# A macaron block on one core: the first expert layer's arrival as a pipeline, three of its batches multiplied beside attention

## The chip, the core and the metric

One core of a Trainium2 chip. The metric is device time of one execution in microseconds (us), the median of several runs. The kernel is written by hand in an explicit order: every engine (TensorE = PE, VectorE = DVE, ScalarE = ACT, GpSimd = POOL, and SyncE = SP, which here only issues transfers) works through its instructions strictly in the order in which the program emits them.

## The reference

x has 8 batches of 512 tokens with 512 channels, float32. Three residual layers follow each other:

```python
x = x + 0.5 * ffn(layernorm(x))
x = x + attn(layernorm(x))
x = x + 0.5 * ffn(layernorm(x))

def ffn(xf):                       # 4096 tokens, 16 experts, one shared weight
    S = softmax(xf @ router_w + router_b)
    G, idx = top_k(S.T, 256)       # each expert takes its 256 best tokens
    out = xf[idx] @ expert_w + expert_b
    return zeros.at[idx].add(G * out)

def attn(x):                       # 16 heads, 4 key/value heads, D = 32, causal
    q, k = rope(x @ Wq), rope(x @ Wk)          # two halves a per head
    s = softmax(mask(q_a . k_a) / sqrt(D))     # a = 0, 1
    diff = softmax(mask(s[0] - lam * s[1]))
    att = rms_norm(diff @ v) * rms_w * 0.2
    return att @ Wo
```

Since all experts share one weight, ffn is one product per token, and a weight per token: the sum of its probabilities over the experts that chose it.

## The kernel before

**Data.** x stays in SBUF as eight tiles `x_sb[b]` of 128 partitions by 4 by 512 (four token tiles i of a batch). `ffn(0)` is the first expert layer, `ffn(1)` the second.

**Arrival (L1019 to L1036).** SP loads x batch by batch, then the choice constants, then attention's weights. For each batch b the loop emits three parts (`arrive`): statistics (`stats`, L236 to L246, DVE and ACT), normalised tiles `xn` (L260, POOL), transposes on PE (L271) that ACT copies to a buffer `y{b}` (L278), router logits (L290), their sums (L303, L310). `expert(count)` puts that many products y x expert weight on PE (L323, four to a token tile), ACT copies the result (L330) and POOL adds the bias row `eb` (L333). Between batches `prepare` lists small work on attention's lambda and output weight (L166 to L188); two of its transfers are asked for in that loop, after all weights.

**Search (`search`, L397 on).** Each expert's threshold is found by 30 bits, one after the other: DVE counts (L420), PE adds the counts over partitions (L424), DVE decides (L427, L428). Beside each bit `expert(per_bit)` keeps PE in work, here 2 or 3 products a bit, and `behind` puts 2 and 4 after the last bit. At the end weights `wt` (L461) say how much of each token's product is added; `update(b, i)` (L464, DVE) does it.

**Preparation (k = -20 to -1).** A table of slots orders this part and attention: `at(o, slot, fn)` places work in block k0 + o, and `fill(k, slot)` emits it. Batch 0 is updated, normalised for attention (`norm_steps`: statistics L488, root L492, shift L496, apply L503, transposes L511) and its first rope products are made (`rope_steps`, PE L563, DVE L572 and L574, a swap of rows by two transfers L580 on SP, POOL L584). The updates of the other seven batches and seven products are spread over its blocks by `PRE_UPDATES` and `PRE_PRODUCTS`.

**Attention (k = 0 on).** 16 phases (batch b, half gp of the heads) of 11 blocks. A block holds 4 x 128 to 4 x 512 scores per partition: `scores` (PE L669, four banks), `energies` (DVE L686: mask added and row minimum), `exps` (ACT L699), in the next block `factors` (L706) and `weigh` (POOL L713 factors, L728 scaling of the odd softmaxes, L735 mask), `difference` (DVE L748), then `exps2` (ACT L762), transposes (`turn_pe` L782, copies L795 on DVE and L797 on ACT), `values` (L810, L825). Rope products and values of the next half, and the output part of the half before (`finish_steps`: squares L599 and L600 on POOL, sums L606, root L617, turned factors `f_f` L625, L633, projection `f_o` L641, residual L647) are placed in slots. The order inside block k:

```python
if u2 is not None: turn_pe(u2)
... values_pe, fill "short", factors, weigh, energies(u)
scores(blocks[k + 1])
... exps2, exps, fill "act mid", fill "mid", turn_copy
fill(k, "long")
... values_out, fill "dve", difference(u1), fill "act", fill "pool"
```

"long" holds the large products on PE (rope, values, projection); what follows them on DVE stands in "mid" of the next block, behind that block's energies. PE has eight PSUM banks: 0 to 3 scores, 4 and 5 transposes, 6 and 7 (`MISC`) in turn for all else.

**Tail.** The second expert layer starts beside the last phase (`EARLY`, `drain`), has its own search with `per_bit` (2,) and `behind` (0, 2), and the outputs leave in 20 transfers.

Of the kernel before, what the change touches and what calls it, by code (L numbers as in the profile page):

```python
# [40 lines left out]
def macaron_kernel(  # L41
# [53 lines left out]


# [14 lines left out]
    def bank(of, name, shape=(P, S)):  # L111
# [6 lines left out]
    PRE_UPDATES = {4: 2, 5: 1, 6: 1, 7: 1, 8: 1, 9: 1, 10: 1, 11: 2, 12: 2, 13: 3, 14: 3, 15: 3, 16: 3, 17: 4}  # L118
    PRE_PRODUCTS = {0: 4, 5: 3}
# [3 lines left out]
        ((0, 0, 1, 1), 1, (2, 2, 3, 3), (3, 3, 4, 4), 5, 6, (5, 6, 7, 8)),  # L123
        ((2, 2, 3, 3), 4, (5, 5, 6, 6), (6, 7, 7, 8), 9, 10, (9, 10, 11, 11)),
# [13 lines left out]
    nlm = keep.tile([P, 2, H], F32, name="nlm")  # L138
    nc.gpsimd.memset(nlm[:, 1, :], -1.0)
    neglam = nlm[:, 0, :]  # L140
# [22 lines left out]
    def lambda_load(n, a, c):  # L163
        def do(pool):
            lqk[n] = [pool.tile([P, H, D], F32, name=f"l{m}t{n}", tag=f"l{m}t") for m in "qk"]
            nc.sync.dma_start(lqk[n][0], a.partition_broadcast(P))  # L166
            nc.sync.dma_start(lqk[n][1], c.partition_broadcast(P))
        return do
# [10 lines left out]
    def lambda_end(wp):  # L179
        nc.gpsimd.tensor_sub(neglam, lsum[1], lsum[0])  # L180
        nc.gpsimd.tensor_scalar(neglam, neglam, -LAM_INIT, None, ALU.add)
# [4 lines left out]
    def scale_wo(q):  # L186
# [8 lines left out]
        0: [lambda_load(0, lq1, lk1)],  # L195
        2: [lambda_products(0)],
        3: [lambda_sums(0), lambda_load(1, lq2, lk2)],
        4: [lambda_exp(0)],
        5: [lambda_products(1), scale_wo_rows],
        6: [lambda_sums(1), scale_wo(0), scale_wo(1)],  # L200
        7: [lambda_exp(1), lambda_end, scale_wo(2), scale_wo(3)],
# [3 lines left out]
    def ffn(f):  # L205
# [3 lines left out]
        buf, mvs, rstds, nmrs, xns, tps, lgps, lgT, lgs, held = ({} for _ in range(10))  # L209
# [4 lines left out]
        def load():  # L214

# [4 lines left out]
            )  # L220
            held["we"] = new("we", "we", [P, EC, E])
# [10 lines left out]
        def stats_tile(b, i):  # L232
            if i == 0:
                mvs[b] = tiny.tile([P, TPB, 2], F32, name=f"mv{f}_{b}", tag="mv")
# [9 lines left out]
        def stats_shift(b):  # L244
            nmrs[b] = tiny.tile([P, TPB], F32, name=f"nmr{f}_{b}", tag="nmr", bufs=3)
            nc.vector.scalar_tensor_tensor(  # L246
                nmrs[b], mvs[b][:, :, 0], -1.0, rstds[b], ALU.mult, ALU.mult
            )

        def stats(b):  # L250
# [3 lines left out]
            stats_shift(b)  # L254

        def normalise(b, tiles=range(TPB), engine=nc.gpsimd):
            first = None
            for i in tiles:
                xns[b, i] = new("xn", f"xn{b}_{i}_", [P, E], bufs=4)
# [919 lines left out]
```

## Time and profile before

| | us |
|---|---|
| median of 7 runs | 1493.42 (1491.14 to 1503.24) |
| profiled execution | 1493.34 |
| its span | 1491.6 |
| arrival, to the last sums | 0 to 80.3 |
| search, to the weights `wt` | 80.3 to 167.3 |
| preparation, to the first energies | 167.3 to 210.9 |
| attention and what lies beside it | 210.9 to about 1303 |
| drain, second search, outputs | 1303 to 1491.6 |

The span runs from the program's first instruction to its last. "Busy" of PE is by records whose ends are modelled; the spacing of their starts tells more. One full product (128x512) is two PE records; a transpose is one. `<-` in a row stands between what is written and what is read, and in brackets stands the idle time of the engine before the row and what ended it. The granted clock is 1.00 or 0.50 at any time; means lie between.

### The profile page before, as it was taken

What the parts mean: (1) busy time and instruction counts of PE and PEld (TensorE: products, weight loads), DVE (VectorE), ACT (ScalarE), POOL (GpSimd) and SP (SyncE); (2) the same over time, 40 slices, a digit from 0 to 9 for tenths busy, and PEclk for the clock granted to TensorE, in tenths of its full rate; (3) what the DMA queues carried; (4) which work ended last, traced back from release to release, by engine and by line L of the source; (5) the groups of instructions that cost most, each with busy time, mean ns of one, the idle gap of its engine ahead of it and who ended that gap; (6) DMA issues with size and microseconds to landing.
All of it is one profiled execution on the core that took longest, in us unless ns stands there. A gap on an engine that the chain in (4) does not pass through costs nothing.

```text
span 1491.6 us, 29871 instructions
## 1 busy us (share of the span) xinstructions
PE 1381.2 (93%) x9496; PEld 780.4 (52%) x9496; DVE 1199.9 (80%) x4440; ACT 1062.5 (71%) x3551; POOL 757.5 (51%) x1241
## 2 busy tenths in 40 slices
PE   6899899999899999999999999999999998999993
PEld 3544444565465555555555555555556555555551
DVE  4345779889989988998899899889988999644467
ACT  3421128988899898889888998988898989733210
POOL 4543435465555655464645555465546455534335
PEclk9999888999999999998999999998999997999996
DMA  9200000000000000000000000000000001000006
GB/s 347 67 0 1 0 36 36 15 23 30 8 30 9 36 2 36 16 22 15 23 19 19 30 8 37 2 36 9 29 16 23 16 23 37 1 5 1 0 1 225
DMA packets 27502, 48.14 MB, mean 32 GB/s; under 512 B 4672, under 2 KB 5968, under 8 KB 27344
## 3 DMA queue, kind: packets, MB, share of 16 engines
q1 hardware_dynamic: 25104, 42.03, 7.8%
q10 hardware_dynamic: 2208, 4.19, 0.8%
q8 instruction: 75, 1.23, 0.3%
q14 instruction: 83, 0.68, 0.1%
q0 software_dynamic: 32, 0.01, 0.0%
HBM read 16.86 MB, written 8.39 MB: 17 GB/s over the span
## 4 chain that ended last, share of the span: by engine, by line
PE 64%; DVE 23%; POOL 3%; ACT 3%; issue 2%; POOLq 1%; DMA 0%; SPq 0%; DVEq 0%; ACTq 0%
PE r_ps L563 13%; PE yps L323 13%; PE sc L669 10%; PE f_o L641 8%; DVE e L686 8%; DVE t L748 6%; PE tp L782 6%; PE av L810 4%; ACT e L699 2%; PE f_ss L606 2%; PE vps L539 2%; DVE eT L795 2%; PE tp L271 2%; PE f_f L625 1%; POOLq L1175 1%
## 5 line engine op out<-in xcount | busy, mean ns | idle before, releaser
L699 ACT ACTIVATE e<-e,nb 128x512 f32<-128x512 f32 (+3 forms) x1024 | 560.4, 551 | 6.9 <-DVE nb L686 2.9
L686 DVE CUSTOM_DVE_ANT_0 e<-sc,mpos 128x512 f32<-128x512 f32 (+3 forms) x1024 | 434.6, 486 | 15.1 <-PE sc L669 7.8
L762 ACT ACTIVATE t<-t,nm 128x512 f32<-128x512 f32 (+3 forms) x512 | 282.2, 554 | 71.8 <-DVE nm L748 71.2
L728 POOL TENSOR_SCALAR e<-e,z,fac 128x512 f32<-128x512 f32 (+3 forms) x512 | 304.7, 607 | 18.3
L669 PE MATMUL sc<-r,r 32*128 32x256 f32 (+3 forms) x2048 | 278.6, 492 | 10.4 <-DVE nb L686 7.2
L748 DVE CUSTOM_DVE_ANT_0 t<-e,fac 128x512 f32<-128x512 f32 (+3 forms) x512 | 254.7, 547 | 13.3 <-POOL e L735 13.2
L323 PE MATMUL yps<-we,y 128*128 128x512 f32 x512 | 248.4, 615 | 0.0
L563 PE MATMUL r_ps<-hT,wq_sb 128*128 128x512 f32 x512 | 236.1, 605 | 0.0
L782 PEld LDWEIGHTS tp<-ident,t 128*128 128x128 f32 x1280 | 154.0, 149 | 112.7 <-issue 36.1
L782 PE MATMUL tp<-ident,t 128*128 128x128 f32 x1280 | 191.5, 291 | 6.4 <-ACT eT L797 5.4
L699 ACT ACTIVATION_READ_ACCUMULATOR e<-e,nb 128x1 f32 x1024 | 194.3, 190 | 0.0
L333 POOL TENSOR_TENSOR y<-y,eb 128x512 f32<-128x512 f32 x64 | 97.8, 1528 | 167.9 <-ACT y L330 146.2
L584 POOL TENSOR_TENSOR r<-r,r_sw 128x512 f32<-128x512 f32 x80 | 101.7, 1279 | 147.0 <-DVE z L706 79.3
L669 PEld LDWEIGHTS sc<-r,r 32*128 32x128 f32 x2048 | 130.2, 195 | 79.5 <-DVE nb L686 55.0
L563 PEld LDWEIGHTS r_ps<-hT,wq_sb 128*128 128x128 f32 x512 | 94.2, 191 | 123.4 <-issue 104.3
L713 POOL TENSOR_TENSOR fac<-z,nlm 128x4 f32<-128x4 f32 (+2 forms) x176 | 36.9, 210 | 232.3 <-DVE z L706 232.3
L330 ACT COPY y<-yps 128x512 f32<-128x512 f32 x64 | 37.4, 585 | 156.7 <-PE yps L323 153.0
L795 DVE COPY eT<-tp 128x512 f32<-128x512 f32 (+1 forms) x176 | 111.8, 635 | 28.1 <-PE tp L782 28.1
L323 PEld LDWEIGHTS yps<-we,y 128*128 128x128 f32 x512 | 90.0, 194 | 84.5 <-issue 81.2
L641 PE MATMUL f_o<-wo_sb,f_an 128*128 128x512 f32 x256 | 126.9, 642 | 0.3
L797 ACT COPY eT<-tp 128x512 f32<-128x512 f32 (+1 forms) x176 | 93.8, 533 | 17.6 <-PE tp L782 17.0
L735 POOL TENSOR_SCALAR_AFFINE_SELECT e<-e 128x256 f32<-128x256 f32 (+1 forms) x224 | 96.0, 439 | 9.4
(110 smaller groups left out, 1630.4 us busy)
## 6 DMA issues: line engine op xcount, KB each, us to landing
r_sw<-r_by SPq DMA_DIRECT2D x160, 128.0 KB, 2.0
x<-in_x_dram SPq DMA_DIRECT2D x7, 1024.0 KB, 14.1
out_dram<-x SPq DMA_DIRECT2D x6, 512.0 KB, 4.0
out_dram<-x ACTq DMA_DIRECT2D x6, 512.0 KB, 4.0
we<-in_expert_w_dram SPq DMA_DIRECT2D x2, 1024.0 KB, 7.2
wq_sb<-in_wq_dram SPq DMA_DIRECT2D x1, 2048.0 KB, 14.2
x<-in_x_dram SPq DMA_DIRECT2D x4, 256.0 KB, 4.6
wo_sb<-in_wo_dram SPq DMA_DIRECT2D x8, 128.0 KB, 2.9
```

What stands on the lines that cost most here:

```text
L323: nc.tensor.matmul(held["yps"], buf[b][:, i, c * P : (c + 1) * P], held["we"][:, c, :], start=(c == 0), stop=(c == EC - 1),)
L563: nc.tensor.matmul(t["ps"], w[:, c, c0 : c0 + P], st["hT"][:, c, :], start=(c == 0), stop=(c == EC - 1),)
L584: return nc.gpsimd.tensor_add(out, out, t["sw"])
L641: nc.tensor.matmul(t["o"], t["an"][:, c, :], wo_sb[:, c // 2, c % 2, :], start=(c == 0), stop=(c == 3),)
L669: nc.tensor.matmul(u["sc"][j][:, r * n : (r + 1) * n], kq[1 + head][j * D : (j + 1) * D, i * P : (i + 1) * P], kq[0][j * D : (j + 1) * D, ...
L686: nc.vector.tensor_tensor_reduce(out=u["e"][:, j, r * n : (r + 1) * n], in0=u["sc"][j][:, r * n : (r + 1) * n], in1=mpos[:, S - n :], scal ...
L699: nc.scalar.activation(e, e, AF.Exp, bias=u["nb"][:, c : c + 1], scale=-1.0, accum_out=u["z"][:, 0, c : c + 1],)
L728: nc.gpsimd.tensor_scalar(e, e, u["z"][:, 1, c : c + 1], u["fac"][:, 0, par, r : r + 1], ALU.mult, ALU.mult,)
L748: u["diff"] = nc.vector.tensor_tensor_reduce(out=u["t"][:, par, s], in0=u["e"][:, 2 * par, s], in1=u["e"][:, 2 * par + 1, s], scale=u["fac ...
L762: nc.scalar.activation(t, t, AF.Exp, bias=u["nm"][:, par, r : r + 1], scale=-1.0, accum_out=z2[:, col : col + 1],)
L782: nc.tensor.transpose(u["tp"][par][:, o : o + P], u["t"][:, par, r * n + c * P : r * n + (c + 1) * P], ident,)
L795: nc.vector.tensor_copy(o, s)
```

## The change

It makes five things different.

1. **Arrival.** The three parts per batch become one pipeline over ten steps: step b emits sums of batch b-2, logits of b-1, apply of b+1, transposes of b, a few products (`BESIDE`: 4 and 2), statistics of b+2. Four banks take the transposes. x1 is loaded before the expert weight, the lambda rows before attention's weights. The shift (L246) goes: the apply subtracts the mean and multiplies.
2. **Search.** `per_bit` (2,) and `behind` (0, 2).
3. **Late batches 4, 5, 6.** Their transposed tiles are kept in `x_sb[b]` itself; their 12 token tiles have no products in arrival and search. A late tile makes four products and one product of a one-row operand that adds the bias, into one bank; SP loads the original x tile again; DVE updates straight from the bank. Five late tiles stand in the preparation, seven in attention, in block 6 of phases 1 to 7. For the latter the expert weight is put in `x_sb[7]`, whose content (already updated) is moved to HBM and comes back in phase 8.
4. **Attention.** `mask` now masks the even softmaxes before `factors`; the factors with lambda are made in place; blocks with four heads use two broadcast multiplies. Squares move from POOL to ACT. "long" is split in two, and scores of the next block stand between or behind the halves in three places (`PLACES`).
5. **Places.** Some positions in `finish_steps`, `EARLY`, `PRE_UPDATES`, `PRE_PRODUCTS` move by a block or so.

```diff
+    LATE = (4, 5, 6)
+    LENT = 7
+    PRE_LATE = (1, 3, 5, 7, 9)
+    LATER = {1: (6,), 2: (6,), 3: (6,), 4: (6,), 5: (6,), 6: (6,), 7: (6,)}
+    BESIDE = {1: 4, 2: 2}
-    PRE_PRODUCTS = {0: 4, 5: 3}
+    PRE_PRODUCTS = {0: 4}
...
-                    xns[b, i], x_sb[b][:, i, :], rstds[b][:, i : i + 1], nmrs[b][:, i : i + 1],
-                    ALU.mult, ALU.add,
+                    xns[b, i], x_sb[b][:, i, :], mvs[b][:, i, 0:1], rstds[b][:, i : i + 1],
+                    ALU.subtract, ALU.mult,
...
+        def late_load(b, i):
+            nc.sync.dma_start(x_sb[b][:, i, :], xt[b][:, i, :])
+
+        def late_pe(b, i):
+            yps = held["late", b, i] = bank(at["y"], f"lps{b}_{i}")
+            for c in range(EC):
+                nc.tensor.matmul(
+                    yps, buf[b][:, i, c * P : (c + 1) * P], held["we"][:, c, :],
+                    start=(c == 0), stop=False,
+                )
+            nc.tensor.matmul(
+                yps, ident[0:1, 0:1].to_broadcast([1, P]), eb_row, start=False, stop=True
+            )
+
+        def late_update(b, i):
+            nc.vector.scalar_tensor_tensor(
+                x_sb[b][:, i, :], held.pop(("late", b, i)), held["wt"][:, i, b : b + 1],
+                x_sb[b][:, i, :], ALU.mult, ALU.add,
+            )
...
+        def late_steps(at, o):
+            b, i = late.pop(0)
+            at(o, "long", lambda: (f0.late_pe(b, i), f0.late_load(b, i)))
+            at(o + 1, "mid", lambda: f0.late_update(b, i))
...
-                first = nc.gpsimd.tensor_mul(t["sq"], st["aT"][i], st["aT"][i])
-                nc.gpsimd.tensor_tensor(t["u"], z2, z2, ALU.mult)
+                nc.scalar.activation(t["sq"], st["aT"][i], AF.Square)
+                nc.scalar.activation(t["u"], z2, AF.Square, scale=RMS_EPS**0.5)
...
-            at(o, "long", lambda: (pe(0), pe(1)))
+            at(o, "long", lambda: pe(0))
+            at(o, "long 2", lambda: pe(1))
...
+        PLACES = (1, 0, 1, 0, 0, 0, 0, 2, 0, 1, 0, 1, 0, 0, 0, 0, 0, 0, 0, 0, 0, 0)
...
             if u1 is not None:
+                mask(u1)
                 factors(u1)
                 weigh(u1)
...
+    for b in range(B + 2):
+        if b > 1:
+            f0.sums_pe(b - 2)
+        if 0 < b <= B:
+            f0.logits_pe(b - 1)
+            f0.logits_put(b - 1)
+        if b + 1 < B:
+            f0.normalise(b + 1, (0, 1), nc.vector if b + 2 == B else nc.gpsimd)
+            f0.normalise(b + 1, (2, 3))
+        if b < B:
+            f0.turn(b, range(TPB))
+        f0.expert(BESIDE.get(b, 0))
+        if b + 2 < B:
+            f0.stats(b + 2)
+        if b > 1:
+            f0.sums_put(b - 2)
+        if b == B:
+            f0.softmax(0)
...
-    f0.search((2, 3), (2, 4))
+    f0.search((2,), (0, 2))
...
+    def lend():
+        if not away:
+            away["x"] = spill.tile([P, TPB, E], F32, name="x_away")
+            nc.sync.dma_start(away["x"], x_sb[LENT])
+            nc.sync.dma_start(x_sb[LENT], expert_w.rearrange("(c p) n -> p c n", p=P))
+
+    def lend_end():
+        nc.sync.dma_start(x_sb[LENT], away["x"])
```

## The prediction

> **What bounds the kernel now.** I read the page first, then busy time by stage, then rows in time order inside each stage.
>
> ```profile
> span 1491.6 us, 29871 instructions
> PE 1381.2 (93%) x9496; PEld 780.4 (52%) x9496; DVE 1199.9 (80%) x4440; ACT 1062.5 (71%) x3551; POOL 757.5 (51%) x1241
> ```
>
> TensorE is 93% busy, but the ends of its records are modelled, so I ask stage by stage. The stages: arrival, search, preparation, attention. Columns: stretch, length, busy time and instructions of PE, PEld, DVE, ACT, POOL, then the granted clock.
>
> ```profile
> 0.00:80.30 80.30, 62.08 (x321) 35.36 (x321) 32.79 (x89) 31.90 (x68) 41.66 (x60) 0.98 0.56 192
> 80.30:167.30 87.00, 86.30 (x257) 42.13 (x257) 50.92 (x169) 13.38 (x24) 32.65 (x27) 1.00 0.00 0
> 167.30:210.90 43.60, 35.20 (x134) 18.40 (x132) 34.70 (x52) 4.49 (x9) 15.78 (x12) 0.84 0.08 31
> 210.90:1303.00 1092.10, 1038.37 (x8052) 600.13 (x8056) 976.71 (x3829) 965.44 (x3350) 589.19 (x1078) 0.94 0.06 21
> ```
>
> The search is PE's own (86.3 of 87.0). In attention PE, DVE (89%) and ACT (88%) run nearly level. Record to record, a full 128x512 product is two records 0.43 us apart, 0.86 us. Summing PE by such spacings gives about 51 of the 67.1 us of the phase 412.6 to 479.7: rope blocks are PE's, but in blocks 4 to 8 of a phase DVE has hardly a gap. There PE has room and DVE has none.
>
> The same line of products, in the bits of the first and of the second search, where the second has 2 products a bit and the first 2 or 3:
>
> ```profile
> 87.90:158.60 70.70, 69.10 (x146) 25.53 (x146) 1.00 0.00 0
> 1399.70:1456.10 56.40, 56.15 (x116) 19.84 (x116) 1.00 0.00 1
> ```
>
> And four rows in time order: a tile load and who waits for it, a POOL wait in the arrival, and DVE held at an output projection:
>
> ```profile
> 0.80 1.80 SPq L1019 DMA_DIRECT2D x<-in_x_dram  x4
> 3.30 0.69 DVE L236 BATCH_NORM_STATS2 s<-x 128x6 f32<-128x512 f32 x1 [2.23 <-DMA x<-in_x_dram]
> 47.58 1.26 POOL L171 TENSOR_TENSOR lqt<-lqt,lkt 128x512 f32<-128x512 f32 x1 [8.18 <-DMA lkt<-in_lk_dram]
> 389.22 0.69 DVE L647 TENSOR_TENSOR x<-x,f_o 128x512 f32<-128x512 f32 x1 [1.83 <-PE f_o L641]
> ```
>
> A 256 KB tile takes 2.5 us from issue to use. DVE, in order, stood 1.83 us because a residual follows a PE projection by one block: late updates will stand in just such a place.
>
> **Arrival: 24.7 us saved.** Products in it fall from 32 to 6: 26 x 0.86 = 22.4 us of PE. What stays is, per batch, transposes 2.1, logits 1.07, sums 0.96: 4.1 us, 4.2 with the evacuations. I place it in order. The first transpose stays at 11.5. The root for batch 1 is now ahead of ACT's copies of batch 0; x1 lands near 12.0 (14.7 less the 2.7 of the megabyte of weights put behind it), four statistics take 3.2, copies end at 18.1, logits at 19.2. Transposes of batch 1 and four products: 24.8. Batch 2 with two products: 30.6. Five batches at 4.2: 51.6. Sums, logits, evacuation, sums of the end: 55.4. Six products 60.6, then 2.6 to the first count: 63.2, where it was 87.9. DVE (3.5 a batch), ACT (3.3) and POOL (3.0) stay under 4.2. POOL's 8.18 us wait goes: the lambda rows are asked for before the weights and used at batch 6; next late is PE itself.
>
> The clock is one uncertainty. It was 0.5 from 49.5 to 52.9, after that wait. But look at 384:
>
> ```profile
> 380.60:384.00 3.40, 3.35 (x34) 2.33 (x34) 3.15 (x15) 3.40 (x13) 3.11 (x5) 1.00 0.03 7
> 384.00:387.40 3.40, 3.40 (x5) 1.32 (x5) 3.26 (x13) 3.36 (x12) 2.01 (x4) 0.50 0.00 0
> ```
>
> Here it halved although PE was 3.35 of 3.40 us busy before, with small transposes and tiled products, which is just what an arrival without products consists of. So I allow four halved stretches of 3.4 us, 1.7 us each: gain 17 to 27. *The Trainium skill ("TensorE: Matmul & The Clock Gate", Part 1) says that the clock halves only after an idle window of about 3.4 us; by that rule the arrival would lose nothing and gain the full 24.7. The row differs, and I follow the row.*
>
> **Search: 14.3 us saved.** 70.7 less 56.4 for the same 29 intervals, DVE's chain being the limit at 2 a bit. Behind the last bit nothing is gained: 8.7 us to the weights in the first search, 8.7 in the second with the new counts.
>
> **Preparation: 16 us lost.** Before, weights at 167.3, ropes from 184.4, attention at 210.9. DVE loses twelve updates of 0.69, but five late tiles come in: each four products and a bias product over one row and 512 columns. No one-row product is in the trace; by the columns it is 0.86, as a full one, so a tile is 4.3 us, five 21.5. PE was idle or waiting for some 10 us here. The chain is DVE's: the second late update stands before the shift (L496) that the normalisation needs. Its reload is behind the lend on SP's queue: x7 away (1 MB, issued near +8.5 us after the weights, 5 us), then the expert weights into its place (5.6 us to landing in the second layer's load), then the reload, landing near +19 to +22 where the shift was done at +8.4. h tiles, two late tiles between the four transposes: ropes start near +35 instead of +17; they then run at full clock, not half, 2.6 us back. Sum +16. If the lend is quicker or hidden, +8; if PE also waits at half clock, +20.
>
> **Attention, seven late tiles: 24 us lost.** One tile at block 6 of phases 1 to 7. In PE's room 4.3 us of products cost little. But DVE's update waits for PE's end, then for SP to reload the tile (2.5): 4.3 + 2.7 = 7.0 us after the scores, and DVE has only about 3.7 us before it (reciprocal, four energies of 0.62, the rest of the block): it stands 3.3. With its own 0.7 that is 4.0, less 0.6 regained where DVE waited anyway: 3.4 a tile, 24 for seven. Behind the standing update are the copy of the transposes, the difference and the next energies, and for them ACT and PE. Ends: 0.7 a tile (5 us) if the wait falls into slack, 7.5 (52) if nothing covers it.
>
> **Attention, the rest: 13 us saved.** The mask now goes before the factors, while POOL waits for the reciprocal (L706). DVE's difference waited for POOL 13.2 us in 25 places (L748 behind L735): I take half, 7. Scores between the halves of the rope products: at 414.5 to 417.2 PE waited for score banks before two ropes; filling that saves about 1.5 in one phase of two, at most 12; I take 10. The squares go from POOL (1.04 each) to ACT: no ACT square is in the trace; its copies of this size take 0.59, exponentials 0.71, with the small one 0.2. 32 x 0.8 = 26 us on an ACT with 12% room; I charge 4, ends 0 and 13. Two broadcast multiplies for eight in 16 blocks are POOL's, off the path. Range of this part: 1 to 21 saved.
>
> **The rest** (the tail's shift, the router load, one reload of x7 in the eighth phase, needed four phases later) I cost at nothing: SP is free there, and the seven reloads come one block after the last rope swaps of a phase (blocks 1 to 5). If any met swaps, 2 to 3 us each.
>
> Sum: -24.7 - 14.3 + 16 + 24 - 13 = -12.0. The profiled execution took 1493.34 (span 1491.6 and 1.7 around it), the median 1493.42: 1481.3 either way. About 0.5% (7.5 us) is what a measurement here can tell from no change: faster is below 1486, slower above 1501.
>
> **Rivals.** *The late updates stall DVE in full (slower).* The place is block 7 of phases 1 to 7, the price per tile. The other terms save 36.0 us, so 5.1 us a tile eats them all, and above 6.2 the kernel is slower by over 0.5%. At 7.5 a tile: +16.5, 1510. For it: in even phases the bank of the late tile is also that of the next turned factors (f_f), so PE waits with DVE; DVE is full there. Against: ACT and PE can run ahead by a block. Chance 0.21.
>
> *The late tiles vanish in the slack.* PE's sum was 51 of 67, and the POOL waits removed lie in those very blocks. At 0.7 a tile, 5 us: 1493.3 - 31 = 1462. Against: DVE has no gap there. Chance 0.22.
>
> *The arrival does not do what it says.* PE at half clock for much of it, or waiting for copies on ACT, 5.6 us a batch instead of 4.2: gain 13, total near 1493, no change. For it: the row at 384. Against: before, with the same small work, only one stretch was halved. Chance 0.17.
>
> My forecast, all terms about as above: 0.40. Faster is this and the second rival, less a little at the edge: 0.60. Same: 0.18. Slower: 0.22. The range goes from just under the second rival, 1460, to 1503, which leaves out the worse half of the first rival and the lower edge of the second.
>
> **What would show it.** The first count at 63 us; its bits 1.94 apart; first energies of attention near 188, with the shift waiting behind a late update; in block 7 of phases 1 to 7 a late update with 2 to 4 us of idle DVE before it, ended by the reload, and phases there 2 to 4 us longer than phases 8 to 14; no L735-like waits before the differences. Wrong if the first count comes after 70, if late updates wait over 5 us, or if attention as a whole is shorter than before.

## The result, and the profile after

The changed kernel takes 1503.08 us (median of 20 runs, 1497.93 to 1509.69) where the kernel before takes 1494.74 (47 runs). The ratio is 1.0054 (1.0043 to 1.0065): 8 us slower, where 12 us faster was forecast. The profiled execution took 1501.66, its span is 8.4 us longer than before:

```profile
span 1500.0 us, 30000 instructions
PE 1388.3 (93%) x9520; PEld 778.7 (52%) x9520; DVE 1194.7 (80%) x4426; ACT 1077.3 (72%) x3603; POOL 746.3 (50%) x1083
```

The shares alone do not tell which engine sets the time. By stage (stretch, length, busy time and instructions of PE, PEld, DVE, ACT, POOL, granted clock), for arrival to the first count, the 29 bit intervals, first update to first energies, and attention to its last energies:

```profile
0.00:84.34 84.34, 59.50 (x288) 36.44 (x289) 36.75 (x94) 29.69 (x64) 75.14 (x58) 0.86 0.55 183
84.34:140.73 56.39, 56.39 (x175) 28.54 (x176) 35.51 (x145) 8.20 (x14) 17.78 (x14) 1.00 0.00 1
147.79:208.25 60.46, 54.63 (x179) 25.55 (x177) 28.95 (x44) 3.92 (x8) 12.35 (x10) 0.92 0.22 78
208.25:1318.50 1110.25, 1059.84 (x8133) 603.83 (x8134) 986.63 (x3845) 989.07 (x3420) 549.47 (x942) 0.96 0.06 23
```

The same stages of the kernel before are 87.9, 70.7, 43.6 and 1095.7 us long. Against before, by the places of the same instructions:

| stage | forecast, us | measured, us |
|---|---|---|
| arrival, to the first count | -24.7 | -3.5 |
| search, 29 bit intervals | -14.3 | -14.3 |
| from the last bit to the first update | 0 | -1.7 |
| preparation | +16 | +16.9 |
| attention | +11 | +14.6 |
| second layer up to its first count | 0 | -2.9 |
| tail | 0 | -0.7 |
| sum | -12.0 | +8.4 |

Of the miss of 20.4 us, 21.2 stand in the first row; the other rows cancel. The first of the prediction's signs of being wrong, a first count after 70 us, came. In the arrival POOL is busy for 75.14 of 84.34 us. POOL in time order, in the middle of the arrival, shows why:

```profile
27.31 4.13 POOL L268 TENSOR_SCALAR xn<-x,mv,rstd 128x512 f32<-128x512 f32 x2
31.41 1.29 POOL L345 TENSOR_TENSOR y<-y,eb 128x512 f32<-128x512 f32 x1
32.67 18.52 POOL L268 TENSOR_SCALAR xn<-x,mv,rstd 128x512 f32<-128x512 f32 x9
```

Nine applies stand back to back, 2.06 us each. The group of this line (ns: least, median, most), the group of the apply in the kernel before, and two rows of the waits of the first 84 us (total, times, longest):

```profile
L268 POOL TENSOR_SCALAR xn<-x,mv,rstd x60: 2062/2075/2347, 9.7 to 1394.8; 128x512 f32<-128x512 f32 x60
```

```profile
L260 POOL TENSOR_SCALAR xn<-x,rstd,nmr x62: 761/769/1029, 10.9 to 1381.8; 128x512 f32<-128x512 f32 x62
```

```profile
PEld tp L279 <- POOL xn L268: 17.7, 15, 1.7
PE tp L279 <- POOL xn L268: 11.1, 9, 1.4
```

With (mult, add) the apply took 0.77 us before. With (subtract, mult) a batch costs POOL 8.3 us, and PE, whose transposes need the tiles, follows at that pace.

In the preparation, SP's queue in time order, and the shift on DVE:

```profile
154.57 0.35 SPq L356 DMA_DIRECT2D x<-in_x_dram  x1
155.64 0.35 SPq L1152 DMA_DIRECT2D x_away<-x  x1
159.91 0.38 SPq L1153 DMA_DIRECT2D x<-in_expert_w_dram  x1
160.39 3.86 SPq L356 DMA_DIRECT2D x<-in_x_dram  x2
```

```profile
166.18 0.75 DVE L371 SCALAR_TENSOR_TENSOR x<-lps,wt,x 128x512 f32<-128x512 f32 x1 [5.86 <-DMA x<-in_x_dram]
167.50 0.16 DVE L527 SCALAR_TENSOR_TENSOR nmr<-mv,rstd 128x4 f32<-128x4 f32 x1
```

The second reload is issued only behind the loan (L1152, L1153), the late update stands 5.86 us for it, and the shift comes 19.7 us after the first update (147.79). A late tile in attention, block 7 of phase 3, some rows of three engines:

```profile
459.91 1.12 PE L366 MATMUL lps<-eb_row,ident 1*128 1x512 f32 x2
460.06 0.33 SPq L356 DMA_DIRECT2D x<-in_x_dram  x1
462.65 0.75 DVE L371 SCALAR_TENSOR_TENSOR x<-lps,wt,x 128x512 f32<-128x512 f32 x1 [3.06 <-PE f_ss L638]
```

PE's four products before these rows (L362) read the place that the reload overwrites; they end at 459.98, and the reload goes out at 460.06. By 462.65, 2.6 us later, it has landed (the twelve reloads take 2.4 to 2.8). The trace names f_ss as the releaser, a product that has nothing to do with this tile. DVE stands 3.06 us (forecast 3.3).

### The profile page after: what moved, and what is told of

Same layout as the page of the kernel before. It is cut to its first block, busy times and chain, and to the rows that moved or that the text cites. A ratio compares the mean times of both kernels' runs of the same rounds, so it can differ in the third digit from the quotient of the medians.

```text
span 1500.0 us, 30000 instructions
## 1 busy us (share of the span) xinstructions
PE 1388.3 (93%) x9520; PEld 778.7 (52%) x9520; DVE 1194.7 (80%) x4426; ACT 1077.3 (72%) x3603; POOL 746.3 (50%) x1083
## 4 chain that ended last, share of the span: by engine, by line
PE 57%; DVE 24%; ACT 8%; issue 3%; POOL 2%; DMA 1%; DVEq 0%; SPq 0%; POOLq 0%; ACTq 0%
PE yps L335 11%; PE r_ps L595 10%; PE sc L700 9%; PE f_o L671 8%; DVE e L717 7%; DVE t L787 7%; ACT e L730 6%; PE tp L821 4%; PE av L849 4%; PE lps L362 3%; PE f_ss L638 2%; PE vps L570 2%; DVE eT L834 2%; POOL xn L268 2%; DVE x L495 1%
## 5 line engine op out<-in xcount | busy, mean ns | idle before, releaser
L787 DVE CUSTOM_DVE_ANT_0 t<-e,z 128x512 f32<-128x512 f32 (+3 forms) x512 | 259.9, 556 | 4.3 <-POOL e L774 3.7
L774 POOL TENSOR_SCALAR e<-e,z 128x256 f32<-128x256 f32 (+2 forms) x384 | 251.2, 665 | 16.7
L821 PEld LDWEIGHTS tp<-ident,t 128*128 128x128 f32 x1280 | 148.8, 145 | 115.0 <-issue 41.0
L335 PE MATMUL yps<-we,y 128*128 128x512 f32 x416 | 201.8, 614 | 0.7 <-ACT y L342 0.7
L821 PE MATMUL tp<-ident,t 128*128 128x128 f32 x1280 | 184.4, 284 | 9.1 <-ACT eT L836 6.7
L751 POOL TENSOR_SCALAR_AFFINE_SELECT e<-e 128x256 f32<-128x256 f32 (+1 forms) x224 | 99.8, 449 | 120.0 <-ACT e L730 119.1
L268 POOL TENSOR_SCALAR xn<-x,mv,rstd 128x512 f32<-128x512 f32 x60 | 124.3, 2087 | 16.6 <-ACT rstd L257 7.9
L342 ACT COPY y<-yps 128x512 f32<-128x512 f32 x52 | 30.4, 585 | 138.8 <-PE yps L335 138.8
L345 POOL TENSOR_TENSOR y<-y,eb 128x512 f32<-128x512 f32 x52 | 67.1, 1290 | 126.4 <-ACT y L342 103.7
L741 POOL TENSOR_TENSOR z<-z,over 128x4 f32<-128x4 f32 (+2 forms) x176 | 36.1, 205 | 188.0 <-DVE z L739 188.0
L335 PEld LDWEIGHTS yps<-we,y 128*128 128x128 f32 x416 | 72.2, 192 | 64.4 <-issue 60.2
```

Of the source, the lines that this page charges most:

```text
L268: ins = engine.tensor_scalar(xns[b, i], x_sb[b][:, i, :], mvs[b][:, i, 0:1], rstds[b][:, i : i + 1], ALU.subtract, ALU.mult,)
L335: nc.tensor.matmul(held["yps"], buf[b][:, i, c * P : (c + 1) * P], held["we"][:, c, :], start=(c == 0), stop=(c == EC - 1),)
L774: nc.gpsimd.tensor_scalar(e, e, u["z"][:, 1, c : c + 1], u["z"][:, 0, c - nr : c - nr + 1], ALU.mult, ALU.mult,)
L787: u["diff"] = nc.vector.tensor_tensor_reduce(out=u["t"][:, par, s], in0=u["e"][:, 2 * par, s], in1=u["e"][:, 2 * par + 1, s], scale=u["z"] ...
L821: nc.tensor.transpose(u["tp"][par][:, o : o + P], u["t"][:, par, r * n + c * P : r * n + (c + 1) * P], ident,)
```

## Experiments

Sixteen kernels ran. Times are medians; a ratio is against runs of the kernel before on the same chip, with its 95% interval. "First count" is the start of the first count's product. The kernel before, run beside each group of them, had medians of 1493.3 to 1495.7, so medians of different experiments compare to about 2 us.

How far one profile can be trusted: e1, e5 and e6 have the same instructions in attention, and it took 1102.5, 1107.1 and 1106.9 us. By block (from one reciprocal of attention to the next; there is one in each block) the view is sharper. Of 154 blocks, 140 agree between e1 and e5 within 0.06 us; of the rest four differ by 1.6 to 1.75. The traces grant the clock in stretches of 3.41 us, full or half, and 1.7 us is half of such a stretch: what work that PE paces loses when the clock is at half for one. So a total that differs by five us shows little, and the same difference in the same block of every phase shows much.

**e1: the old apply in the changed kernel.**

```diff
+            stats_shift(b)
...
-                    xns[b, i], x_sb[b][:, i, :], mvs[b][:, i, 0:1], rstds[b][:, i : i + 1],
-                    ALU.subtract, ALU.mult,
+                    xns[b, i], x_sb[b][:, i, :], rstds[b][:, i : i + 1], nmrs[b][:, i : i + 1],
+                    ALU.mult, ALU.add,
```

> The changed kernel with one thing undone: the apply multiplies by the root and adds the shift again (the shift is back on DVE), as in the kernel before; pipeline, late tiles and attention stay. Theory A (POOL's subtract-multiply takes 2.08 us a tile instead of 0.77, so that a batch costs POOL 8.3 us and the arrival goes at POOL's pace): POOL falls to 3.1 us a batch, PE is next at 4.2, first count at 63 to 67 instead of 84.3, total 1481 to 1486, faster than before. Rival B (PE at half clock, or waiting for ACT's copies, sets the arrival and POOL only trails it): first count stays at 78 to 84, total 1497 to 1503.

1486.28 us, ratio 0.9939 (0.9917 to 0.9961): faster than before, as theory A had it. But the first count is at 75.1, between the two theories: the apply was the first limit, not the only one. Rows of one batch, in time order (others between them are left out):

```profile
45.48 0.16 DVE L261 SCALAR_TENSOR_TENSOR nmr<-mv,rstd 128x4 f32<-128x4 f32 x1 [3.69 <-ACT rstd L257]
45.56 0.22 DVE L326 TENSOR_TENSOR l<-lg,rb_sb 128x64 f32<-128x64 f32 x1
45.93 1.04 PE L319 MATMUL lg<-sum,lgT 128*128 128x16 f32 x8 [1.64 <-DVE l L326]
48.39 3.08 PE L286 MATMUL tp<-ident,xn 128*128 128x128 f32 x16
50.45 1.75 ACT L294 COPY x<-tp 128x512 f32<-128x512 f32 x3 [0.28 <-PE tp L286]
52.09 0.31 ACT L256 ACTIVATE rstd<-mv,ln_eps 128x4 f32<-128x4 f32 x1
52.73 0.16 DVE L261 SCALAR_TENSOR_TENSOR nmr<-mv,rstd 128x4 f32<-128x4 f32 x1 [3.75 <-ACT rstd L257]
```

Read them as a ring: the shift waits for ACT's root; the evacuation of the sums (L326) stands behind the shift on DVE; PE's next sums wait for that one bank; PE's transposes, ACT's copies of them and ACT's next root follow. One round is 7.25 us here, part of it at half clock (47.3 to 50.7). The shift that the change took out closes this ring. With the same instructions in the arrival, e7 and e8 below have their first counts at 71.5 and 71.7, so the 75.1 is good to some 3 us only.

**e2: the new apply alone in the kernel before.**

```diff
-            stats_shift(b)
...
-                    xns[b, i], x_sb[b][:, i, :], rstds[b][:, i : i + 1], nmrs[b][:, i : i + 1],
-                    ALU.mult, ALU.add,
+                    xns[b, i], x_sb[b][:, i, :], mvs[b][:, i, 0:1], rstds[b][:, i : i + 1],
+                    ALU.subtract, ALU.mult,
```

> The kernel before with the new apply form alone (subtract the mean, multiply by the root; no shift); nothing else of the change. Theory A: POOL's row of the apply goes from 0.77 to about 2.08 us a tile; 30 tiles add 39 us to a POOL that was busy for 41.7 of the first 80.3 us, so the arrival becomes POOL's and the first count moves from 87.9 to 95 to 112; total 1500 to 1518. Rival (the form is slow only beside the busier DVE of the pipeline): the row stays under 1 us and the total within 5 us of before.

1515.88 us, ratio 1.0134 (1.0097 to 1.0171). The row is 2.07 us, the first count at 99.8 instead of 87.9, and attention 10.7 longer. Of that, 5.1 are in the last phase, beside which the second layer's first batches are applied; the rest is mostly in block 1 of odd phases, which depends on the clock (see e10) and not on the form. The slow form needs nothing else of the change.

**e3: six pairs of operations on POOL.**

```diff
+                ops = {1: (ALU.mult, ALU.add), 2: (ALU.subtract, ALU.mult), 3: (ALU.add, ALU.mult),
+                       4: (ALU.mult, ALU.mult), 5: (ALU.mult, ALU.subtract), 6: (ALU.add, ALU.add)}
```

> The kernel before, with another pair of operations in the first layer's apply for batches 1 to 6 (its values are therefore not the reference's; only the rows of the apply are read): 1 (mult, add), 2 (subtract, mult), 3 (add, mult), 4 (mult, mult), 5 (mult, subtract), 6 (add, add). Four POOL tiles each. If the subtraction makes the form slow, batches 2 and 5 take 2.08 us and the others 0.77. If it is the order (a product after a sum), 2 and 3 take 2.08 and the rest 0.77. If only (mult, add) and (mult, mult) have a quick way, 2, 3, 5 and 6 are slow.

POOL's rows in time order, batches 1 to 6, four tiles each, and behind them a single multiplication of the same shape, which is a row of the kernel before too (L188):

```profile
18.23 3.03 POOL L263 TENSOR_SCALAR xn<-x,rstd,nmr 128x512 f32<-128x512 f32 x4 [6.02 <-DVE nmr L246]
...
27.94 8.26 POOL L263 TENSOR_SCALAR xn<-x,rstd,nmr 128x512 f32<-128x512 f32 x4 [3.89 <-DVE nmr L246]
...
37.43 3.02 POOL L263 TENSOR_SCALAR xn<-x,rstd,nmr 128x512 f32<-128x512 f32 x4
...
49.23 3.03 POOL L263 TENSOR_SCALAR xn<-x,rstd,nmr 128x512 f32<-128x512 f32 x4
...
53.45 8.27 POOL L263 TENSOR_SCALAR xn<-x,rstd,nmr 128x512 f32<-128x512 f32 x4
...
62.93 8.29 POOL L263 TENSOR_SCALAR xn<-x,rstd,nmr 128x512 f32<-128x512 f32 x4
...
78.09 3.15 POOL L188 TENSOR_SCALAR wo_sb<-wo_sb,rms_sb 128x512 f32<-128x512 f32 x2
```

None of the three rules that I had written down fits. (mult, add), (add, mult) and (mult, mult) take 0.76 us a tile; (subtract, mult), (mult, subtract) and (add, add) take 2.07; a product alone 1.57. All six have the same operands and the same shape, so the pair itself decides, and (add, mult), which serves a mean whose sign is turned, is a quick one.

**e4: no late tiles in attention.**

```diff
-            for o in LATER.get(ph, ()):
-                late_steps(at, o)
-            if ph == max(LATER) + 1:
-                lend_end()
...
-            if len(updates) == TPB * (LENT - 1 - len(LATE)):
-                lend()
```

> The changed kernel without the seven late tiles in attention (their products, reloads and updates are left out, and with them the loan of the x7 tile; the values of those seven tiles are not the reference's). The prediction's term (3.4 us a tile): 24 us shorter, 1479. Stretches of the two traces by phase (3.7 to 4.4 a tile): 1472 to 1477, phases 1 to 7 down to those of before. Rival (they lie in slack, 0.7 a tile): 1498. In the preparation the reload no longer stands behind the loan on SP's queue: a few us shorter there if the loan held it up, 0 if the late updates themselves did.

1477.34 us, ratio 0.9881 (0.9856 to 0.9905). The total fits the phases' reading only because two parts add: attention is 18.2 us shorter than in the changed kernel, 2.6 a tile, and the preparation 8.1 (52.4 instead of 60.5), the price of the loan on SP's queue. Without late tiles attention is still only 3.6 us shorter than before. By block the price of a tile is higher: block 7 of phases 1 to 7 is 3.5 to 5.4 us shorter than in the changed kernel, and in the odd ones block 8 gives 1.1 to 1.4 back, 24.8 in all or 3.5 a tile (against e1, which has half clock in fewer of these blocks, 22.3 or 3.2). The other 6.6 us are lost elsewhere, much of them in steps of 1.7: e4's attention has 133 us at half clock, the changed kernel's 82.

**e5: e1 with the ring cut.**

```diff
-        if b + 2 < B:
-            f0.stats(b + 2)
         if b > 1:
             f0.sums_put(b - 2)
+        if b + 2 < B:
+            f0.stats(b + 2)
```

> The kernel of e1 with one line moved in the arrival: DVE evacuates the sums of batch b-2 before the statistics and the shift of b+2, not after. Reading of e1's trace: there PE's sums wait for their one bank, which DVE frees only behind the shift, which waits for ACT's root, which stands behind ACT's copies of the transposes that PE has just made: a ring of four engines, 5.8 to 7.6 us a batch. Theory A: with the ring cut PE sets the pace again, 4.2 to 5 us a batch; first count at 64 to 69 (e1: 75.1), total 1476 to 1480. Rival B (PE's halved clock or x's arrival set e1's pace): first count stays within 2 us of 75, total 1485 to 1488.

1476.59 us, ratio 0.9869 (0.9850 to 0.9888); first count at 63.7. PE in time order:

```profile
33.14 1.97 PE L286 MATMUL tp<-ident,xn 128*128 128x128 f32 x16
...
36.94 1.97 PE L286 MATMUL tp<-ident,xn 128*128 128x128 f32 x16
...
40.78 1.97 PE L286 MATMUL tp<-ident,xn 128*128 128x128 f32 x16
```

A batch is 3.8 us, PE's own, and the mean clock over the arrival is 1.00 (e1 0.93, the changed kernel 0.86). Theory A holds. Rival B falls: e5 has the same transfers, and the half clock goes with the waits.

**e6: e5 with the loan behind the last reload of the preparation.**

```diff
-            if len(updates) == TPB * (LENT - 1 - len(LATE)):
+            if k == -20 + max(PRE_LATE) + 1:
                 lend()
```

> The kernel of e5 with the loan of x7 (its way out and the expert weights' way in) issued on SP behind the last reload of the preparation instead of ahead of the second. Theory A (the second late update, and the shift behind it, wait for a reload that stands behind the loan on SP's queue): the stretch from the first update to the first energies falls from 61 to 52 to 54 us, where PE's own work is next; total 7 to 9 below e5. Rival (late tiles' products on PE set that stretch, the loan is hidden): within 2 us of e5.

1469.57 us, ratio 0.9820 (0.9801 to 0.9839), 7.0 below e5. The preparation, first update to first energies:

```profile
126.80:180.90 54.10, 52.36 (x179) 24.54 (x177) 29.08 (x45) 3.92 (x8) 11.10 (x10) 0.97 0.26 88
```

PE is busy for 52.36 of 54.10: the loan was what kept it waiting, and next is its own work, the late products among it.

**e7: e1 without the reloads in attention.**

```diff
-            at(o, "long", lambda: (f0.late_pe(b, i), f0.late_load(b, i)))
+            back = len(late) >= len(LATE) * TPB - len(PRE_LATE)
+            at(o, "long", lambda: (f0.late_pe(b, i), back and f0.late_load(b, i)))
```

> The kernel of e1 without the reload of the seven late tiles in attention (their updates read what lies there, so the values of those tiles are not the reference's); products and updates stay. By the prediction's account (DVE stands because the reload's 2.5 us follow PE's end: 3.3 us of 3.4 a tile) the stand falls to 0.8 and a tile costs 0.7 to 1.5: attention 10 to 15 us shorter, total 1471 to 1476. Rival (the 4.8 us of products on PE, or the bank that they hold, are what a tile costs, and the reload's wait is covered): attention within 4 us, total 1482 to 1487.

1477.24 us, ratio 0.9888 (0.9860 to 0.9916), 9 below e1. In the profile attention is 6.8 us shorter, 1.0 a tile, and DVE's idle time before the late updates of attention is PE's alone:

```profile
its engine sat idle before it (us, times) until:
  DMA x<-in_x_dram: 20.6, 4
  PE lps L373: 8.9, 7
```

(The four are the preparation's.) The stand fell from 3.0 to 1.3 us (means of seven). By block, block 7 of the seven phases got 1.0 to 1.35 shorter, 8.2 us together; the rest are steps of the clock. So a tile got only 1.0 to 1.2 cheaper, and neither account holds as written: this much of a tile is the reload, the rest PE's products (4.7 us of PE in every one) and the update itself.

**e8: the squares back on POOL.**

```diff
-                nc.scalar.activation(t["sq"], st["aT"][i], AF.Square)
+                first = nc.gpsimd.tensor_mul(t["sq"], st["aT"][i], st["aT"][i])
...
-            at(o0, "act", square)
+            at(o0, "pool", square)
```

> The kernel of e1 with the squares of the output part back on POOL (as in the kernel before). The prediction charged 4 us for having them on ACT (ends 0 and 13): by that the total falls to 1482 (1473 to 1486). Rival (ACT has room there and POOL had not): 1487 to 1492.

1488.52 us, ratio 0.9956 (0.9936 to 0.9976), which can't be told from e1. On ACT a square takes 0.63 us, and these 32 cost nothing that shows; the 4 us charged for them did not appear, within the 2 us or so that medians tell.

**e9: the mask late again, in e6.**

```diff
-                mask(u1)
                 factors(u1)
                 weigh(u1)
+                mask(u1)
```

> The kernel of e6 with the mask back behind the scaling of the odd softmaxes on POOL (the order of the kernel before, but still on the even ones). The prediction's term (mask early saves 7 us, half of the 13.2 us that differences waited for POOL): 1476 to 1477. Rival (those waits were covered by others): within 3 us of 1469.6.

1473.05 us, ratio 0.9856 (0.9838 to 0.9874). The differences wait for POOL again, 6.3 us in 17 places (e6: none), but attention is only 0.6 us longer. The medians say 3.5 us, with intervals that just touch. In any case less than the 7 of the prediction: most of what DVE waits there does not lengthen attention.

**e10: the scores' places undone, in e6.**

```diff
-        PLACES = (1, 0, 1, 0, 0, 0, 0, 2, 0, 1, 0, 1, 0, 0, 0, 0, 0, 0, 0, 0, 0, 0)
+        PLACES = (0, 0, 0, 0, 0, 0, 0, 0, 0, 0, 0, 0, 0, 0, 0, 0, 0, 0, 0, 0, 0, 0)
```

> The kernel of e6 with the scores of the next block always ahead of the large products (all PLACES 0), as in the kernel before. The prediction's term (scores between the halves save 10 us, at most 12): 1479 to 1481. Rival (PE's order moves DVE's wait from one place to another): within 3 us of 1469.6. With e9: what the prediction called the rest of attention (13 saved) came out at about 6, so one of the two must fall short.

1486.76 us, ratio 0.9935 (0.9911 to 0.9960): 17 us. Its twelve runs spread from 1479.9 to 1496.5 where e6's four lie between 1467.6 and 1470.0. In the profile attention is 18.5 longer, 16.7 of it in phases 0, 3 and 7. The start of phase 3 in e10, in stretches of 3.4 us, and a like stretch of e6:

```profile
390.60:394.00 3.40, 3.38 (x12) 2.02 (x13) 2.12 (x7) 3.40 (x18) 0.71 (x1) 0.50 0.00 0
394.00:397.40 3.40, 3.40 (x5) 1.35 (x4) 2.76 (x17) 3.40 (x12) 2.83 (x5) 0.51 0.03 7
```

```profile
391.20:394.60 3.40, 3.38 (x14) 1.70 (x12) 3.40 (x18) 3.40 (x12) 2.82 (x5) 1.00 0.01 2
```

With the scores put ahead of all rope products the clock is at half for two stretches in which the big rope products run; with the places it stays full. Block 1, where these products stand, is 4.3 to 4.5 us longer in phases 0, 3 and 7; in phases 1, 9, 11 and 13, with the same order but full clock there, only 0.4 to 0.6 (1.9 in phase 5, where the half clock reaches in for 0.6 us). The three phases have 17.9 us more at half clock than in e6, which can account for 9 of the 16.7 at most. So neither order nor clock alone makes the loss: the old order is expensive where the clock is at half. The kernel before, e2 and e3, whose attention has the old order too, agree: block 1 of an odd phase takes 8.7 to 9.1 us at full clock and 11.6 to 12.7 with 2.4 to 3.9 at half, in phases 7 and 13 of one trace, 3, 7 and 11 of the next, 1 and 11 of the third. With the places it takes 8.25 in every trace but for phase 1 of e4 and e15 (8.61, 8.54); in phase 1 of e13 it takes 8.26 although 3.4 us of it are at half clock.

**e11: late updates in attention in slot dve, in e6.**

```diff
-            at(o + 1, "mid", lambda: f0.late_update(b, i))
+            at(o + 1, "mid" if f0.held["we"] is not x_sb[LENT] else "dve", lambda: f0.late_update(b, i))
```

> The kernel of e6 with the seven late updates in attention a few instructions later on DVE: in slot dve of the same block (behind the two copies of the transposes, ahead of the difference) instead of mid. Reading of e6's block 7: DVE stands for 3.2 us, about 1.5 of it for PE's products and 1.7 for the reload; behind the copies the reload has landed, and the stand shrinks to what PE needs, about 2.2. Theory A (the reload is worth about 1 us a tile, as e7 measured): 5 to 8 us less, 1462 to 1465. Rival (the copy that goes first waits for transposes that PE makes only behind the late products, so that the stand only changes its name): within 3 us of 1469.6.

1467.22 us, ratio 0.9809 (0.9791 to 0.9828); attention as long as in e6. The rows of phase 3:

```profile
431.95 0.56 DVE L841 COPY eT<-tp 128x384 f32<-128x384 f32 x1 [1.95 <-PE tp L828]
433.09 0.75 DVE L378 SCALAR_TENSOR_TENSOR x<-lps,wt,x 128x512 f32<-128x512 f32 x1 [0.59 <-DMA x<-in_x_dram]
```

The update now waits 0.59 us (3.16 in e6), but the copy ahead of it 1.95 for PE's transposes. The stand changed its place: the rival.

**e12: late products split over blocks 5 and 6, in e6.**

```diff
+            at(o - 1, "long", lambda: f0.late_pe(b, i, (0, 1)))
+            at(o, "long", lambda: (f0.late_pe(b, i, (2, 3)), f0.late_load(b, i)))
```

> The kernel of e6 with the late products of attention split: two products in block 5, two and the bias product in block 6; reload and update where they were. PE ends 1.8 us earlier in block 6 and the reload starts earlier. Theory A (what a late tile costs, 2.6 us, is DVE's stand behind PE's end and the reload): the stand falls from 3.2 to 1.4 a tile, 8 to 12 us less, 1458 to 1462. Rival (what a tile costs is PE's own 4.8 us in blocks where PE has little room, so block 5 pays what block 7 saves): within 3 us of 1469.6.

1471.59 us, ratio 0.9835 (0.9815 to 0.9856), attention 0.4 us shorter: the rival again. The stand did fall, from 3.0 to 1.6 us a tile, but block 7 got only 0.3 us shorter a tile. DVE's stand is not what a tile costs.

**e13: the kernel before with the places of the scores and the halves alone.**

```diff
+        PLACES = (1, 0, 1, 0, 0, 0, 0, 2, 0, 1, 0, 1, 0, 0, 0, 0, 0, 0, 0, 0, 0, 0)
...
-            at(o, "long", lambda: (pe(0), pe(1)))
+            at(o, "long", lambda: pe(0))
+            at(o, "long 2", lambda: pe(1))
...
             fill(k, "long")
+            if place == 1:
+                scores_next(k)
+            fill(k, "long 2")
```

> The kernel before with one part of the change: the large products in two halves, and the scores of the next block between or behind them in the places of PLACES. The prediction's term: 10 us saved, at most 12: 1484 to 1487, with the blocks 1 of phases 0, 1, 7, 13, 14 (10.3 to 11.9 us there against 9.0 in like phases) back at 9. If the 17 us that e10 lost by the same places hold here too: 1477 to 1480. Rival (the places only mend what the late tiles and the moved output parts bring about): within 3 us of before.

1479.89 us, ratio 0.9923 (0.9903 to 0.9943): 11 to 13 us. Attention is 14.1 shorter; block 1 of phases 0, 7 and 13, which the expectation named, loses 3.4 to 3.8 each, and these are the blocks that are at half clock in the trace of before. So the places gain without the late tiles too, and a little more than the 10 of the term. But they do not gain as the term was added up, 1.5 us in one phase of two: in phase 3, where the prediction saw PE wait, block 1 loses 0.74.

**e14: the output parts at their old block numbers, in e6.**

```diff
-                    finish_steps(at, (0, 1, 1, 3, 4), b - 1, 2, sts[b - 1])
+                    finish_steps(at, (0, 1, 1, 4, 5), b - 1, 2, sts[b - 1])
...
-                finish_steps(at, (4, 5, 5, 8, 9), b, 0, sts[b])
-                finish_steps(at, (6, 7, 7, 9, 10), b, 1, sts[b])
+                finish_steps(at, (4, 5, 5, 7, 9), b, 0, sts[b])
+                finish_steps(at, (6, 7, 8, 9, 10), b, 1, sts[b])
```

> The kernel of e6 with the output parts back at the block numbers of the kernel before: (0, 1, 1, 4, 5), (4, 5, 5, 7, 9) and (6, 7, 8, 9, 10). Theory (these moves, which the prediction costed at nothing, are what ate the rest of attention's gain: block 8 of odd phases is 2.0 us longer than before without any late tile, block 7 only 1.35 shorter, and the end of block 10 up to 1.7 longer): 4 to 10 us less, 1460 to 1466. Rival (they make way for the late tile's bank, so that without them PE waits for that bank in block 7 and 8): 3 to 15 us more, 1473 to 1485.

1467.48 us, ratio 0.9833 (0.9807 to 0.9860). The profiled execution, the fastest of four, has attention 5.9 us shorter; the medians show no difference. By block the theory has half of it right. Block 8 of phases 9, 11 and 13 falls from 6.4 to 6.7 us, 3.7 to 4.3 of them at half clock, to 4.8 at full clock; block 10 falls by 1.4 to 1.7 in six odd phases, again with the half clock gone. Block 7 grows by 9.6 us over all phases, which speaks for the rival. What the moves are worth in all is not settled.

**e15: the changed kernel with the quick pair.**

```diff
+            if done[b] == TPB:
...
+                nc.vector.tensor_scalar(negs[b], mvs[b][:, :, 0], -1.0, None, ALU.mult)
...
-                    xns[b, i], x_sb[b][:, i, :], mvs[b][:, i, 0:1], rstds[b][:, i : i + 1],
-                    ALU.subtract, ALU.mult,
+                    xns[b, i], x_sb[b][:, i, :], negs[b][:, i : i + 1], rstds[b][:, i : i + 1],
+                    ALU.add, ALU.mult,
```

> The changed kernel with one thing different: DVE writes the mean with its sign turned (128x4 elements, straight behind the statistics, no wait for ACT), and the apply adds it and multiplies by the root. e3 showed (add, mult) at 0.76 us a tile on POOL, so the shift need not come back. Theory (two causes, POOL's form, and in e1 the ring through the shift; this removes both without touching the order): POOL 3.0 us a batch, first count at 62 to 66, total 1474 to 1480, about e5. Rival (the order of the sums' evacuation matters also without the shift, since it stands behind four statistics): first count at 70 to 76, total 1483 to 1488, about e1.

1480.49 us, ratio 0.9910 (0.9876 to 0.9944); first count at 62.7. The group of the apply:

```profile
L272 POOL TENSOR_SCALAR xn<-x,neg,rstd x60: 762/768/1037, 9.9 to 1366.1; 128x512 f32<-128x512 f32 x60
```

Only this is different from the changed kernel, and it is worth some 22 us. Neither the shift nor another order is needed. This is the change as the prediction had priced it: forecast 1481.3 and a first count at 63.

**e16: e15 with the loan of e6 and the slot of e11.**

```diff
+            if k == -20 + max(PRE_LATE) + 1:
                 lend()
...
+            at(o + 1, "mid" if f0.held["we"] is not x_sb[LENT] else "dve", lambda: f0.late_update(b, i))
```

> The kernel of e15 with the loan of x7 behind the last reload of the preparation (as in e6) and the seven late updates in slot dve (as in e11). If these add: 8 us less than e15 by the loan, 0 to 3 by the slot: 1464 to 1471.

1468.89 us, ratio 0.9831 (0.9797 to 0.9865). The loan's gain adds to it. e6, e11, e14 and e16 lie between 1467 and 1470 and can't be told apart; all beat both kernels by 25 us and more.

## Why the prediction was wrong, and where it was right

**The step that failed** is in the arrival: "DVE (3.5 a batch), ACT (3.3) and POOL (3.0) stay under 4.2." The 3.0 was four tiles at 0.77, the row of the old pair, given to a new pair with no bound on either side. It measures 8.3, so the arrival is POOL's: -3.5 instead of -24.7. The trace of before held a warning: a single multiplication of the same shape took 1.57 us, twice the pair with one operation more, so POOL's time did not follow the shape alone:

```profile
L188 POOL TENSOR_SCALAR wo_sb<-wo_sb,rms_sb x4: 1557/1566/1583, 74.4 to 83.8; 128x512 f32<-128x512 f32 x4
```

The slow pair also costs about 2.4 us in the last phase and 1.8 in the second layer up to its first count (changed kernel against e1). The third rival came nearest to this stage (13 gained there instead of 24.7), but by other engines. The half clock that it named was there, 24 us of the changed kernel's arrival; with the quick pair it is gone but for 3.4 us at most (e5, e15), so it followed from the waits for POOL and was not the cause.

**Right:** nearly all else of the arrival. With the quick pair it ends 25.2 us earlier than before (87.9 to 62.7, e15), against 24.7 forecast, and from batch 1 on PE sets the pace. The products of batch 2 end at 30.8 us (forecast 30.6). That it agrees to 0.5 us is partly luck: five batches take 3.9 each and not 4.2, and the end, from the last transposes to the first count, takes a us more than forecast. That removing the shift mattered I had not seen: with it, but in the new order, the engines form a ring (first count 71.5 to 75.1 in e1, e7 and e8, 63.7 in e5).

**The clock in the arrival.** I had allowed four halved stretches, for the row at 380.6. e5 shows none, e15 one (17.4 to 20.8, behind a wait of PE of 3.34 us): small transposes without waits kept full clock. The Trainium skill ("TensorE: Matmul & The Clock Gate", Part 1) would have it so, and for these two its outcome was the better one. The changed kernel does not fit its idle window of about 3.4 us. Two stretches of its arrival, one behind the other:

```profile
64.23:67.64 3.41, 2.22 (x20) 1.67 (x22) 0.00 (x0) 1.43 (x3) 3.41 (x2) 1.00 0.02 5
67.64:71.06 3.42, 3.42 (x20) 2.41 (x13) 0.00 (x0) 1.58 (x3) 3.42 (x4) 0.50 0.00 0
```

The clock halves though PE was busy for 2.22 of the 3.41 us before. At all eight places where it halves in the arrivals of the changed kernel and e1, PE was busy for 0.9 to 2.2 us of the stretch before, and no single wait there was over 1.8 us. So short waits were enough, without a stretch that was idle. In attention the halved stretches stay (e10), some behind stretches in which the records show PE busy for 2.97 (e10) or 3.35 (the row at 380.6) of 3.40 us; no run here shows what sets those off.

**POOL by the page.** In e15's row a quick pair takes 0.768 us for 512 elements in each partition. The Trainium skill ("GPSIMD Engine Reference", section 3.1) gives 769 ns measured for 512 elements in the best case, which agrees; for the 2.07 of the other pairs it has no figure.

**Search and preparation:** -14.3 and +16.9 for -14.3 and +16. The mechanism of the preparation (shift behind a late update, its reload behind the loan) is the one in the rows, and e6 and e4 show its size: 6 to 8 us is the loan's (6.0 in e6, 8.1 in e4). What is left, 52 to 54 us, PE is busy with, the late products among it.

**Late tiles:** forecast 3.4 us each; measured 3.2 to 3.5 in the tile's own block and the next, 2.6 over attention as a whole (e4). DVE's stand was right too (3.06 for 3.3). But that the price came out is in part luck, for it is not the stand: with 1.7 us of it gone the tile is 1.0 to 1.2 cheaper (e7), with 1.4 of it gone 0.3 (e12), and moving the update gains nothing (e11). The sentence that fails is "In PE's room 4.3 us of products cost little": they take 4.7, and what is left of the price without the reload is PE's products and the update. How it divides between these two is not shown.

**Rest of attention:** forecast -13, measured -3.6 (14.6 less the 18.2 of the late tiles), or -6 without the slow pair's 2.4. By parts: places 10 forecast, 11 to 17 measured (e13, e10); squares 4 charged, 0 measured (e8); mask 7 forecast, 0 to 4 measured (e9). These sum to more than -6, so something costed at nothing takes part of it back. By block it shows where: blocks 8 and 10 of the odd phases 1 to 13 are together 14 us longer in the changed kernel than before (20 in e4), with part of them at half clock; in e14, with the old positions of the output parts, they are 0.7 us shorter than before. So the moved output parts lengthen these blocks. But they shorten others, so what the moves cost in all stays open, and the broadcast factors and the factors made in place were not tried alone.

**Not foreseen, small:** 1.7 us behind the last bit, 2.9 in the second layer, both in the change's favour; no run here takes them apart.

## What to carry to other kernels

Price an instruction by a row of its own operations, not of its shape: two pairs of operations on the same shape differed by 2.7 times on POOL, and that alone turned a gain of 14 us (e15) into a loss of 8. Where a pipeline has a single evacuation bank, look at what stands ahead of the evacuation on its engine, and follow that back round: a small dependent instruction there can close a ring over several engines. A stand of 3 us on a full engine is not yet 3 us of time, and moving it within the phase gained nothing. Compare two traces block by block and not by their totals: the totals of equal instructions differed by 5 us here, single blocks by 0.06.

## What was not expected of the hardware

POOL's two-operation scalar form on 128x512 float32: 0.76 us for (mult, add), (add, mult), (mult, mult); 2.07 for (subtract, mult), (mult, subtract), (add, add); 1.57 for mult alone. The clock halved behind stretches of 3.41 us in which PE was busy for up to 2.2 us, without a wait over 1.8 (arrivals of the changed kernel and e1). With the old order of scores and rope products, a half clock at the start of an odd phase goes with 3 to 4 us more in its first block (before, e2, e3, e10), in other phases from trace to trace; with the places of the scores that block took 8.25 to 8.61 us in every trace.
